# Carrying the count of later neighbours inside the mask chunks of a graph layer

## The chip, the core and the metric

The kernel runs on one core of one Trainium2 chip. Its engines work side by side and wait for one another through semaphores: TensorE (PE, matrix products into the accumulators of PSUM, eight banks), VectorE (DVE), ScalarE (ACT), GpSimd (POOL) and SyncE (SP, which here only issues DMAs). Each engine works through its own instructions in the order in which they were written, and a DMA belongs to the queue of the engine that issues it. The metric is the device time of one execution in microseconds, as the median of the runs.

## The reference

Four graph layers over 4096 nodes with 64 features share one adjacency matrix of 0 and 1 (about one entry in a thousand is 1). Each layer adds to `x` what it computes from `h = max(layernorm(x), 0)`. Layer 0 is an attention with sigmoid scores, masked by the adjacency; layer 2 forms `A h`; layer 3 the mean over the neighbours and a product with a weight matrix. The change concerns layer 1:

```python
support = input @ weight
mask = (adj != 0).astype(support.dtype)
rank = jnp.cumsum(mask, axis=1)
deg = rank[:, -1:]
k = jnp.minimum(deg, 100.0)
pos = rank - (deg - k)
w = mask * jnp.where(pos > 0, 0.5 ** (k - pos), 0.0)
out = w @ support + bias
```

So a neighbour's weight is 0.5 to the power of the number of neighbours that come after it in its row, and nothing if a hundred or more do.

## The kernel before

The adjacency lies transposed in memory, neighbours on the partitions. A block `ib` is 512 of the nodes (8 blocks, `IB`); a chunk `t` is 128 of the possible neighbours (32 chunks, `NT`). In layer 0 POOL's DMAs bring the matrix in as fp8, one tile `masks[ib]` of 128 x 32 x 512 per block, and the later layers use these tiles. Since they hold exact values only for an adjacency of 0 and 1, DVE also checks every chunk in fp32: `check(2)` (L347) issues a load of two chunks (`ckw`, 512 KB) on SP and puts the comparison on DVE; four buffers let the loads run ahead. Should one entry be odd, a general version (`model(True)`) runs afterwards; it doesn't here. A list of checks is worked off in layers 0 to 3 wherever the program calls for one; what is left before the end is done in `done3` (L1545).

*Work in small pieces.* What belongs to the rows of a block (norms, splits, transposes) is written as generators. `push` puts one into a queue with a lag and `step()` (L312) moves each one piece on; the loops of products call `step()` at fixed places. So all engines' instructions have a fixed order, and `manual_schedule` keeps it.

*Layer 1* computes the weights from counts. With h split in two fp16 parts (`s2a`, written by `rows0`), it needs for each chunk and block the number of later neighbours of every entry:

1. `chunks_counted` (L1188) counts, for four blocks at a time (a `quad`), the neighbours in each of the 32 chunks: 128 narrow products into one bank, 32 rows per block. Every eighth chunk it may call a check and calls `step()`. ACT copies the counts into `many` (L1313) and, half by half, into a second tile in which the halves are exchanged (L1317).
2. The loop at L1334 goes through four pairs of blocks, chunks from the last to the first, two chunks a step, so four units (block, chunk) a step and 16 steps a pair. `counted` (L1253) makes for each unit a full product `after` x mask (L1260), 128 times 100 for the entry itself less 128 for every later one in the chunk. Behind the four of them stands a second product for each (L1270), which subtracts the later chunks' counts: its weights are one column of `later` broadcast, 32 rows high, so the four use different rows of the PE array. The units of a step are chosen, with the exchanged tile, so that they do.
3. `weights` (L1277) turns each count into int16, negative ones into 0, on ACT or DVE: the second unit always on DVE, the fourth in every fourth step. Read as bf16 the integer is the power of two that is wanted. The five banks in `COUNTS` take the counts in turn, so a new count waits until the one five units before it has been read.
4. `products` (L1293) multiplies the step before's weights with `s2a` into one of two banks per pair (L1298); after the last chunk ACT evacuates the sum and `rows1` (L1166) goes on with the block's rows.

The loop's line L1343 asks for a check in three of four steps (none in the first four). Layer 2 and 3 are run by `sums` (L1386): 256 products each, a `beat()` (L1360) after every four, with `step()` and, by the pattern `often`, a check. In layer 2 the pattern is two in five; layer 3 begins with one in three and goes over to two in three 24 beats later. `rows2` (L1410) norms the rows for layer 3 and transposes them on PE (L1435), which reads what DVE wrote (L302).

## Time and profile before

| | us |
|---|---|
| median of 3 runs | 595.43 (595.21 to 595.67) |
| span of the profiled execution | 593.2 |
| PE busy in it | 577.5 |
| DVE busy | 477.9 |
| ACT busy | 337.7 |
| layer 1, counting of the chunks | 297.5 to 312.1 |
| layer 1, loop from the first products on | 314.8 to 458.6 |
| layer 2 | 458.6 to 523.8 |
| layer 3 and the end | 523.8 to 593.2 |

Of the profiled execution the span is known: the time from its first to its last instruction; what a run takes besides is the difference to the times of the runs. A row of a group or of the timeline names the engine, the line (L1260), the operation, what it writes and reads (`cnt<-mask,after`), the shapes and how often; then follow its time and, in brackets or behind a bar, the idle time before it with what ended it. PEld is PE's loading of weights, SPq SP's queue. A window's row gives each engine's busy time in it, PEclk the share of the clock that TensorE was granted, and the DMA engines' share. Idle time of an engine costs only where another one waits for it.

### The profile page before, as it was taken

To read this page: it belongs to the slowest core of one execution; us is meant where nothing else is said; L and a number is where in the kernel's file an instruction comes from. 1 tells how busy PE (TensorE), PEld (TensorE's weight loads), DVE (VectorE), ACT (ScalarE), POOL (GpSimd) and SP (SyncE) were. 2 spreads that over 40 slices of the span, in tenths; PEclk is the share of its full clock that TensorE was granted. 3 is DMA by queue.
4 is the path that set the end of the run, shared out by engine and by line. 5 is a ranking of instruction groups with operands and counts; after the bars stand their busy time and mean duration, and the time that the engine had idled before them with its cause. 6 is when DMAs were issued, how large, how long until landed. Compare 5 with 4: busy or idle time off the path is not lost.

```text
span 593.2 us, 9215 instructions
## 1 busy us (share of the span) xinstructions
PE 577.5 (97%) x3138; PEld 238.6 (40%) x3138; DVE 477.9 (81%) x909; ACT 337.7 (57%) x546; POOL 242.7 (41%) x459
## 2 busy tenths in 40 slices
PE   8999999999999999999999999999998999999995
PEld 3663333333333333333243343343443545544553
DVE  5679666899989899999876878879888669987753
ACT  3678666667676776767427677767666014431221
POOL 7625204657767676744434201001010305562352
PEclk9999999999999999999999999999999999999999
DMA  9995932898999899962191545555555486546921
GB/s 148 131 106 45 102 30 18 82 151 136 168 150 166 144 158 153 149 145 88 42 349 38 173 153 189 167 173 177 166 191 181 151 271 200 161 172 210 312 83 42
DMA packets 43016, 87.04 MB, mean 147 GB/s; under 512 B 5136, under 2 KB 22032, under 8 KB 42960
## 3 DMA queue, kind: packets, MB, share of 16 engines
q1 hardware_dynamic: 23808, 68.40, 35.3%
q0 software_dynamic: 18720, 17.57, 31.8%
q8 instruction: 26, 0.43, 0.3%
q10 hardware_dynamic: 432, 0.40, 0.3%
q14 instruction: 30, 0.25, 0.1%
HBM read 135.63 MB, written 1.05 MB: 230 GB/s over the span
## 4 chain that ended last, share of the span: by engine, by line
PE 77%; DVE 10%; POOL 6%; issue 3%; ACT 3%; DMA 1%; DVEq 0%; POOLq 0%; ACTq 0%
PE acc L1370 19%; PE ps L938 12%; PE acc L969 11%; PE acc L1298 10%; PE cnt L1260 9%; DVE att L962 4%; PE cnt L1270 3%; PE idle L1062 3%; PE many L1193 2%; PE pt L236 2%; POOL mask L180 1%; PE pr L1173 1%; POOL rs_a L265 1%; DVE ck L361 1%; PE pn L1447 1%
## 5 line engine op out<-in xcount | busy, mean ns | idle before, releaser
L361 DVE SCALAR_TENSOR_TENSOR ckw<-ckw 128x1024 f32<-128x1024 f32 x98 | 124.5, 1278 | 5.5 <-DMA ckw<-adjt_dram 5.3
L938 PE MATMUL ps<-qt,kt 64*128 64x512 f32 x512 | 123.2, 610 | 2.9 <-DVE att L962 2.5
L969 PE MATMUL acc<-att,fb 128*64 128x512 f32 x512 | 117.8, 599 | 0.6 <-DVE att L962 0.5
L1286 ACT ACTIVATE w<-cnt 128x512 int16<-128x512 f32 x176 | 93.1, 597 | 42.3 <-PE cnt L1270 41.9
L962 DVE TENSOR_TENSOR att<-ps,mask 128x1024 f32<-128x1024 f32 x82 | 98.4, 1217 | 8.4 <-ACT ps L951 8.3
L951 ACT ACTIVATE ps<-ps,att_c,att_a 128x1024 f32<-128x1024 f32 x82 | 93.5, 1177 | 1.5 <-PE ps L938 1.3
L951 ACT ACTIVATE att<-ps,att_c,att_a 128x1024 f32<-128x1024 f32 x46 | 54.6, 1203 | 59.0 <-PE ps L938 58.8
L180 POOL DMA_DIRECT2D mask<-adjt_dram x128 | 70.1, 558 | 19.7 <-DMA mask<-adjt_dram 18.2
L938 PEld LDWEIGHTS ps<-qt,kt 64*128 64x128 f32 x512 | 45.1, 186 | 77.9 <-issue 32.9
L1284 DVE TENSOR_SCALAR w<-cnt 128x512 int16<-128x512 f32 x80 | 53.6, 687 | 23.2 <-PE cnt L1270 21.8
L962 DVE TENSOR_TENSOR att<-att,mask 128x1024 f32<-128x1024 f32 x46 | 56.6, 1246 | 18.1 <-ACT att L951 18.1
L1260 PE MATMUL cnt<-mask,after 128*128 128x512 fp8e4 x256 | 66.3, 379 | 1.9 <-DVE w L1284 1.4
L1298 PE MATMUL acc<-w,s2a 128*128 128x512 bf16 x256 | 66.5, 382 | 0.1
L280 POOL TENSOR_TENSOR xc<-x_sb,st 128x256 f32<-128x256 f32 x24 | 20.0, 832 | 110.1 <-DVE st L277 70.8
L969 PEld LDWEIGHTS acc<-att,fb 128*64 128x64 f32 x512 | 33.5, 136 | 73.0 <-issue 67.5
L1370 PE MATMUL acc<-mask,s2a 128*128 128x512 fp8e4 x256 | 57.8, 379 | 0.0
L1370 PE MATMUL acc<-mask,s2b 128*128 128x512 fp8e4 x256 | 57.7, 379 | 0.0
L265 POOL TENSOR_TENSOR rs_a<-rs_y 128x4 f32<-128x4 f32 x48 | 18.2, 378 | 69.2 <-DVE rs_y L261 66.7
L361 DVE SCALAR_TENSOR_TENSOR ck<-ck 128x512 f32<-128x512 f32 x60 | 43.1, 718 | 0.0
L1260 PEld LDWEIGHTS <-after 128*128 128x128 bf16 x256 | 24.8, 99 | 30.8 <-issue 3.4
L1370 PEld LDWEIGHTS <-s2b 128*128 128x128 f16 x256 | 25.0, 98 | 27.6 <-issue 0.8
L1370 PEld LDWEIGHTS <-s2a 128*128 128x128 f16 x256 | 24.6, 98 | 27.3
(198 smaller groups left out, 606.3 us busy)
## 6 DMA issues: line engine op xcount, KB each, us to landing
ckw<-adjt_dram SPq DMA_DIRECT2D x98, 512.0 KB, 3.5
mask<-adjt_dram POOLq DMA_DIRECT2D x128, 128.0 KB, 9.0
ck<-adjt_dram SPq DMA_DIRECT2D x60, 256.0 KB, 5.9
x_sb<-x_dram SPq DMA_DIRECT2D x4, 256.0 KB, 7.7
out_dram<-y POOLq DMA_DIRECT2D x6, 128.0 KB, 2.2
out_dram<-y ACTq DMA_DIRECT2D x2, 128.0 KB, 2.2
w_sb<-wts_dram SPq DMA_DIRECT2D x2, 80.0 KB, 7.6
vec<-vecs_dram ACTq DMA_DIRECT2D x1, 130.5 KB, 6.3
```

The source lines that it names most:

```text
L180: nc.gpsimd.dma_start(out=masks[ib][:, g * CG : (g + 1) * CG, :], in_=adjt[ib, g])
L265: nc.gpsimd.tensor_tensor(a, y, y, ALU.mult)
L361: nc.vector.scalar_tensor_tensor(at, at, 0.0, at, ALU.not_equal, ALU.not_equal, accum_out=odd[:, k : k + 1])
L938: nc.tensor.matmul(ps[:, c, :], kt[half, g, :], qts[ib][half, :], start=True, stop=True)
L951: nc.scalar.activation(to, ps, AF.Sigmoid, bias=att_c, scale=att_a)
L962: nc.vector.tensor_tensor(att, frm, mask, ALU.mult)
L969: nc.tensor.matmul(acc[c * D : (c + 1) * D, :], lhs[:, t, :], rhs[:, c, :], start=(at == 0), stop=(at == NG - 1), skip_group_check=True,)
L1260: nc.tensor.matmul(cnt, after, masks[ib][:, t, :], start=True, stop=True, skip_group_check=True)
L1284: nc.vector.tensor_scalar(w, cnt, 0.0, None, ALU.max)
L1286: nc.scalar.activation(w, cnt, AF.Relu)
L1298: nc.tensor.matmul(accs[ib], both(s2a, t), w, start=(t == NT - 1), stop=False, skip_group_check=True,)
L1370: nc.tensor.matmul(acc, both(s2, t), masks[ib][:, t, :], start=(t == 0), stop=(t == NT - 1), skip_group_check=True,)
```

## The change

The last two rows of every mask chunk (126 and 127, `LANES`) no longer hold neighbours in layer 1 but two fp8 numbers whose sum is the number of later neighbours, up to 120; `after` has -128 in these rows, so the one product with the mask subtracts them too and the row-tiled product goes. The rows taken out form a 33rd chunk `apart_m` per block (32 chunks x 2 rows, and beneath them the same numbers again), with its own matrix `apart` and its own features `apart_s`. In detail:

- `taken`: for each of the 8 blocks two DMAs on SP copy the two rows (512 bytes x 32 chunks on one partition) to 32 partitions of `apart_m`, at the start of layer 1.
- `numbered`, per quad, replaces the second ACT copies: PE forms the later counts (`beyond` x `many`, and four `pair` products that add the taken rows), DVE makes the two fp8 numbers, and 16 DMAs on SP write them into the mask rows and `apart_m`. Quad 0's runs during the second `chunks_counted`, quad 1's in the loop's first three steps.
- The loop runs over 33 chunks in steps of four units (66 units a pair, so a last step of two); a check comes in every second step from the sixth on, over all pairs. `features_apart` copies two rows of `s2a` by two DMAs when all blocks' features are ready.
- `given_back`: after each pair two DMAs per block restore the mask rows for layers 2 and 3.
- Layer 2's checks go from two in five beats to one in two; the remaining ones before the flag come one a step.
- The constants grow in `count_constants`: small POOL operations, with one more `yield`; `later` goes.

```diff
@@ count_constants
-    nc.vector.tensor_scalar(later[lanes, :], tri[lanes, lanes], -128.0, None, ALU.mult)
+    nc.gpsimd.tensor_scalar(beyond[lanes, lanes], tri[lanes, lanes], 1.0, None, ALU.mult)
...
+            nc.vector.memset(after[:, KEPT:P], 0.0)
...
@@ flagged
+            steps = 7
+            while checks:
+                check(2)
+                steps = max(steps - 1, 3)
+                yield
...
@@ chunks_counted(quad, meanwhile)
                     step()
+                    next(meanwhile, None)
...
+        def lanes_of(ib, n):
+            return masks[ib][KEPT + n : KEPT + n + 1, :, :]
+
+        def taken(ib):
+            for n in range(LANES):
+                nc.sync.dma_start(out=apart_m[n * NT : (n + 1) * NT, ib, :], in_=lanes_of(ib, n))
+
+        def given_back(ib):
+            for n in range(LANES):
+                nc.sync.dma_start(out=lanes_of(ib, n), in_=apart_m[n * NT : (n + 1) * NT, ib, :])
+
+        def numbered(quad):
+            pn = pm.tile([P, IB], F32, tag="pr", name=f"pn_{quad}{sfx}")
+            nc.tensor.matmul(
+                pn, beyond, many[quad], start=True, stop=False, skip_group_check=True
+            )
+            for q in range(QUAD):
+                nc.tensor.matmul(
+                    pn[q * NT : (q + 1) * NT, :], pair, apart_m[:, quad * QUAD + q, :],
+                    start=False, stop=q == QUAD - 1, skip_group_check=True,
+                )
+            yield
+            two = work1.tile([P, LANES, IB], FP8, name=f"two_{quad}{sfx}")
+            nc.vector.tensor_scalar(two[:, 0, :], pn, MOST, None, ALU.min, saturate=False)
+            nc.vector.scalar_tensor_tensor(
+                two[:, 1, :], pn, MOST, two[:, 0, :], ALU.min, ALU.subtract,
+                saturate=False,
+            )
+            yield
+            for q in range(QUAD):
+                ib = quad * QUAD + q
+                rows = slice(q * NT, (q + 1) * NT)
+                for n in range(LANES):
+                    nc.sync.dma_start(out=lanes_of(ib, n), in_=two[rows, n, :])
+                    to = slice((LANES + n) * NT, (LANES + n + 1) * NT)
+                    nc.sync.dma_start(out=apart_m[to, ib, :], in_=two[rows, n, :])
+
+        def features_apart():
+            for n in range(LANES):
+                nc.sync.dma_start(
+                    out=apart_s[n * NT : (n + 1) * NT, :],
+                    in_=s2a[KEPT + n : KEPT + n + 1, :, :, :].rearrange("p t k d -> p t (k d)"),
+                )
@@ counted
+                by, what = (apart, apart_m[:, ib, :]) if t < 0 else (after, masks[ib][:, t, :])
+                nc.tensor.matmul(cnt, by, what, start=True, stop=True, skip_group_check=True)
...
-                nc.tensor.matmul(
-                    cnt, later[lanes, t : t + 1].to_broadcast([NT, P]),
-                    many[ib // QUAD][other][lanes, :],
-                    start=False, stop=True, skip_group_check=True,
-                )
@@ the loop
+            nc.gpsimd.memset(apart_m[LANES * NT : P, :, :].bitcast(I32), 0)
+            nc.gpsimd.memset(apart_s[LANES * NT : P, :], 0.0)
+            for ib in range(NIB):
+                taken(ib)
...
             for blocks in GROUPS:
-                for k in range(NT // PAIR):
-                    t = NT - 1 - k * PAIR
-                    units = [(ib, t - n) for n in range(PAIR) for ib in blocks]
-                    cnts = counted(units)
-                    ws = weights(units, cnts, k)
+                units = [(ib, t) for t in reversed(range(-1, NT)) for ib in blocks]
+                for at in range(0, len(units), CI):
+                    now = units[at : at + CI]
+                    cnts = counted(now)
+                    ws = weights(now, cnts, k)
                     if late is not None:
                         products(*late)
-                    late = units, ws
-                    if k % 4 != 1 and (blocks != GROUPS[0] or k >= 4):
+                    late = now, ws
+                    if k % 2 and k >= 4:
                         check(2)
+                    k += 1
                     step()
+                    next(numbers, None)
+                    if not moved and len(ready.get(1, ())) == NIB:
+                        features_apart()
+                        moved = True
+                if not general:
+                    push(giving(blocks), 2)
...
-        made, beats, often = [0], [0], [True, False, True, False, False]
+        made, beats, often = [0], [0], [True, False]
...
-                    while checks:
-                        check(2)
```

## The prediction, made before the change was run

> **What bounds the kernel now.** I read the page first: TensorE (PE) is busy for nearly the whole span, and the chain that ended last is 77% PE.
>
> ```profile
> span 593.2 us, 9215 instructions
> ...
> PE 577.5 (97%) x3138; PEld 238.6 (40%) x3138; DVE 477.9 (81%) x909; ACT 337.7 (57%) x546; POOL 242.7 (41%) x459
> ...
> PE 77%; DVE 10%; POOL 6%; issue 3%; ACT 3%; DMA 1%; DVEq 0%; POOLq 0%; ACTq 0%
> ```
>
> That share is a mean over stages, so next the stages: layer 1's loop, from its first products to layer 2, and the second half of layer 2.
>
> ```profile
> core 0: us, PE busy (x) PEld busy (x) DVE busy (x) ACT busy (x) POOL busy (x), PEclk, DMA share, GB/s
> 314.80:458.60 143.80, 141.82 (x806) 56.08 (x803) 121.13 (x232) 101.00 (x196) 18.07 (x33) 1.00 0.51 165
> ...
> 488.00:523.80 35.80, 35.80 (x206) 18.83 (x205) 34.22 (x75) 14.71 (x43) 19.84 (x22) 1.00 0.58 180
> ```
>
> PE sets the loop, with VectorE (DVE) at 84% behind it; in layer 2's second half both are full. Then one step of the loop, in order of time:
>
> ```profile
> 343.05 1.04 PE L1298 MATMUL acc<-w,s2a 128*128 128x512 bf16 x4
> ...
> 343.93 1.03 PE L1260 MATMUL cnt<-mask,after 128*128 128x512 fp8e4 x4
> ...
> 344.88 0.10 PEld L1270 LDWEIGHTS <-later 32*128 32x128 bf16 x4 [0.42 <-issue]
> 344.89 0.39 PE L1270 MATMUL cnt<-many,later 32*128 32x512 bf16 x4
> ...
> 345.21 1.04 PE L1298 MATMUL acc<-w,s2a 128*128 128x512 bf16 x4
> ```
>
> A step lasts 345.21 - 343.05 = 2.16 us. A full product takes 0.216 us (in layer 2 twenty in a row took 4.32), so four counts and four products are 1.73 and the row-tiled set is the remaining 0.43: its four run side by side, but their weights load only 0.1 before them and the next weights wait for them.
>
> Then the queue that the change loads, SyncE's (SP): a line's DMA rows, and its first issues of layer 1.
>
> ```profile
> L357 SPq DMA_DIRECT2D ckw<-adjt_dram x98: 327/328/430, 295.4 to 564.0; - x98
> DMA to landing us min/median/max: 3.1/3.5/6.5
> ...
> 295.43 1.75 SPq L357 DMA_DIRECT2D ckw<-adjt_dram  x4
> ```
>
> An issue takes 0.33 us and four come in 1.75: 0.44 each. Last, how closely layer 2's PE follows DVE: the normed rows and the transposes that read them.
>
> ```profile
> 508.37 0.42 DVE L302 SCALAR_TENSOR_TENSOR sup<-xc,rs 128x256 f32<-128x256 f32 x1
> ...
> 514.43 0.42 DVE L302 SCALAR_TENSOR_TENSOR sup<-xc,rs 128x256 f32<-128x256 f32 x1
> ...
> 520.50 0.42 DVE L302 SCALAR_TENSOR_TENSOR sup<-xc,rs 128x256 f32<-128x256 f32 x1
> ```
>
> ```profile
> 509.40 0.38 PE L1435 MATMUL ph<-ident,sup 128*128 128x128 f32 x2
> ...
> 515.16 0.38 PE L1435 MATMUL ph<-ident,sup 128*128 128x128 f32 x2
> ...
> 521.07 0.41 PE L1435 MATMUL ph<-ident,sup 128*128 128x128 f32 x2
> ```
>
> DVE needs 6.06 us a block, PE 5.76, and PE's lead shrinks: from the end of `sup` to the transpose 0.6, 0.3, 0.15 us. There is no slack left for more DVE work.
>
> **The change, part by part.** The sum is made against the profiled span, 593.2; the median of the runs, 595.43, is 2.2 above it, which I take as unchanged.
>
> *Opening of layer 1.* `taken` puts 16 DMAs on SP ahead of the checks' loads: 16 x 0.44 = 7.0 us. Their target lies, by the order of the pools, where layer 0's `kt` was, whose last reader ends at 288.4; SP's last `ck` load goes out at 286.6. So they end at 295.4, just when the first `ckw` load went out before (295.43): nothing, if that reading holds (else the third rival). The memsets on POOL (0.31 for 256 columns, so some 1.2) fall into its idle 296.1 to 303.5. PE then meets `numbered(0)` behind the first four matmuls of the second count: ACT's copy of the counts ended at 305.9, PE is there at 305.4, and five matmuls follow: +1.1, so the counts end at 313.2 instead of 312.1. The two DVE operations stand behind `xc` (L302), which waited for POOL's rsqrt and ended at 309.98; at 0.65 each (the `w` row has 0.687) they end at 311.3. SP issues from 311.4: the first block's second lane is the third DMA (312.2), the second block's the seventh (314.0); landing is taken as 2.2 (the `out_dram` row, the only one from SBUF), so PE may count at 314.4 and 316.2. Four counts, `numbered(1)`'s 0.6, four counts: first products at 318.4 instead of 314.8. **+3.6.** Bounds: +1.7 (only PE's own work) to +5.5 (0.6 an issue, the small L82 loads' row, and 3.1 to land, the `ckw` row's least).
>
> *The loop.* 62 more sets of 0.43 go: **-26.7**; the 33rd chunk adds 8 counts and 8 products of 0.216: **+3.5**.
>
> *SP's queue in the first steps.* `numbered(0)`'s 16 issues last till 318.4. `numbered(1)`'s DVE part runs behind step 1's two `w`, to 320.5; its 16 issues end at 327.6. The load for the check of step 5 is next in that queue: it lands 3.5 later, 331.1. DVE, in order, reaches that check at 326.3 (steps of 1.73) and stands 4.8; behind it is step 6's `w`, ready at 332.8, and its bank is what step 7's third count takes, due at 328.4: **+4.4**. Bounds: 0 (if DVE's slack and shorter issues cover it) and 7.5 (0.6 an issue). `features_apart` does the same again: it waits on SP for the last `s2a` (step 12), two issues, then the load of step 13's check lands 4.4 after `s2a` while DVE is there after 2.0; the bank ring covers 0.4: **+2.0** (0 to 2.5). `given_back` puts four issues (1.8 us) behind each pair of blocks; the loads run four checks, eight steps of 1.73, ahead, which covers it; without that cover DVE waits up to those 1.8 a group.
>
> *DVE and ACT at the faster step.* Thirteen checks at 1.2 leave the loop: DVE has 121 - 16 + 4 = 109 of some 120 us, ACT 101 + 2 (DVE and ACT get four more `w` each for the 33rd chunk, at 0.6 and 0.5; DVE also 1.3 for `numbered(1)`). A step with two `w` and a check is 2 x 0.61 + 1.14 = 2.4 of DVE against 1.73, the next 0.6; five banks let a `w` be 0.8 late. Row work of 2.85 a block lands on top, and at each pair's end two evacuations (1.27 of ACT) meet the next pair's first products, without a row-tiled set between. The loop had 143.8 - 108.9 - 26.7 - 5.8 (row matmuls) = 2.4 of waits; I take 4.5, **+2.1**: nearer the lower end (-2.4) since the slack covers most, the upper being all row work of six blocks uncovered, +15.
>
> *Layers 2 and 3.* They get the 13 checks. Layer 2's 64 beats carry 32 instead of 25; in the stretch from 488 a cycle of five beats gets 2.5 instead of 2, four more in all, at 1.55 each (1.63 and 1.53 beside POOL, 1.22 alone): 6.2 us on a full DVE, less the 0.5 of lead: **+5.7**. Their loads are hidden: the DMA engines are 58% busy there, and a load is issued four checks ahead. Bounds 0 and 7 x 1.55 = 10.9. Layer 3's six lie beside PE, whose transposes there wait for ACT's copies; the last check comes nine beats later, near 574, `flagged` still sums seven steps before its product, and the flag was written at 582: nothing; if DVE lags by more, what passes 582.
>
> *Layer 0.* Thirteen small POOL operations (0.19 as L267) and three memsets (0.1 to 0.23), 3 us, fall into POOL's idle 109.3 to 113.4; DVE loses four of 0.17 in a place (108.6 to 110.2) that the chain passes: **-0.3** (-0.7 to +1). The four ACT copies that go (0.62) were off the path: nothing.
>
> Sum: 3.6 - 26.7 + 3.5 + 4.4 + 2.0 + 2.1 + 5.7 - 0.3 = -5.7: span 587.5, time **589.7**.
>
> *Rule against row.* The Trainium skill, "TensorE: Matmul & The Clock Gate", Part 3, has row-tiled matmuls running side by side, four ending some 4 ns apiece after one. By it a set would cost 0.22, the loop would save 13.6, and the sum would be +7, slower; this trace shows 0.43 a set, which decides. The skill's "SBUF — State Buffer", Door 1, puts partitions 124 to 127 on one of 16 DMA ports, of 435 GB/s together: an estimate of 0.6 us for each 16 KB lane; `taken` would last 9.6 instead of 7.0 us and the sum would be -3; no row here shows a transfer from one partition.
>
> **The rivals.**
> - *The queue waits are hidden and layer 2 keeps up* (loads early enough, DVE's extra checks in its idle time of early layer 2): the 4.4, 2.0 and most of the 5.7 go: 578 to 585. For it: DVE idles 10 us from 458 to 488. Against it: order in a queue is fixed, and the stretch from 488 is full.
> - *DVE and ACT become the loop's bound*: a step of 1.85 instead of 1.73 over 66 steps, +8 on the sum: 594 to 600. For it: DVE at 91% with lumps of 2.4; against: 13 checks fewer.
> - *Slower: SP's queue at the opening.* If `apart_m` is free only when the last gather ends (295.4), the 7.0 us of `taken` stand before the first `ckw`: the checks on DVE, `xc` behind them, both numbers and their DMAs come 6.6 later, so 589.7 + 6.6 = 596.3, and with issues of 0.6 instead of 0.44 (2.6 more on `taken`, 3 on step 5) 602. It decides from a delay of 7 us. For it: the first `ckw` load itself waited for that gather. Against: its pool lies further up, over `att`.
>
> **How the numbers follow.** Forecast 0.45 (585 to 594), hidden 0.17, DVE and ACT 0.15, SP's queue 0.23. A measurement tells 0.2%, 1.2 us, from no change: faster is below 594.2, the first two, 0.62; same is where the last two begin, 0.08; slower the rest, 0.30. Leaving out a tenth at each end gives 580 to 602. Low are the hidden case's middle, high the slower rival's end.
>
> **What would show it.** A step of 1.73 us without L1270; PE idle some 3 us before the first counts, released by a DMA; DVE waiting for `ckw` loads near steps 5 and 13; transposes L1435 that wait for `sup` in layer 2, and a longer layer 2. I'm wrong if the 16 `taken` issues begin after 295, if DVE doesn't wait for `ckw` in the loop, if the step stays near 2 us, or if PE's idle time lowers the granted clock: it stayed 1.00 over 1.7 us of idle at 295.4.

## The result and the profile after

The changed kernel is slower: 620.43 us median of 4 runs (618.69 to 623.11) against 595.55, a ratio of 1.0417, 95% interval 1.0391 to 1.0444. The forecast was 589.7, with 602 as its upper end. The profiled execution has a span of 617.0 us (before 593.2). From the same marks in both traces, with the forecast's own terms beside them:

| stretch | before | after | difference | forecast |
|---|---|---|---|---|
| up to the first counting product | 297.5 | 298.1 | +0.6 | -0.3 |
| opening: counting to the loop's first products | 17.3 | 38.2 | **+20.9** | +3.6 |
| loop of layer 1 | 143.8 | 133.4 | -10.5 | -14.7 |
| layer 2 | 65.2 | 69.5 | +4.3 | +5.7 |
| layer 3 and the end | 69.4 | 77.8 | **+8.4** | 0 |
| span | 593.2 | 617.0 | +23.8 | -5.7 |

The page of the changed kernel: PE was busy for 97% before, now for 91%, and the chain that ended last, 77% PE before, is 47% PE; the rest is other engines, DMAs and queues.

```profile
span 617.0 us, 8858 instructions
...
PE 562.3 (91%) x2916; PEld 240.1 (39%) x2916; DVE 482.4 (78%) x914; ACT 337.4 (55%) x546; POOL 257.3 (42%) x477
...
PE 47%; DVE 21%; POOL 10%; issue 7%; DMA 7%; ACT 4%; SPq 3%; DVEq 0%; POOLq 0%; ACTq 0%
```

The stretches by windows (busy time of each engine, PE's granted clock, DMA share): the opening's late part, the loop, the second half of layer 2, layer 3 up to the flag, and the end.

```profile
core 0: us, PE busy (x) PEld busy (x) DVE busy (x) ACT busy (x) POOL busy (x), PEclk, DMA share, GB/s
314.80:336.30 21.50, 4.62 (x13) 1.24 (x14) 10.01 (x21) 3.32 (x7) 11.01 (x29) 0.60 0.20 68
336.30:469.70 133.40, 121.37 (x578) 56.80 (x577) 106.22 (x208) 100.75 (x197) 14.14 (x27) 0.99 0.38 131
503.50:539.20 35.70, 31.95 (x182) 16.32 (x180) 34.15 (x77) 13.71 (x41) 24.63 (x22) 1.00 0.68 232
539.20:602.00 62.80, 57.93 (x300) 28.62 (x298) 48.67 (x92) 15.45 (x40) 26.47 (x25) 1.00 0.67 228
602.00:617.00 15.00, 7.48 (x30) 3.44 (x30) 4.33 (x14) 0.47 (x1) 2.02 (x3) 0.75 0.10 33
```

In 314.8 to 336.3, where the kernel before had PE busy throughout, PE worked for 4.6 of 21.5 us, at 0.60 of its clock. In the loop it was idle for 12 of 133 us. The opening in order of time, first SP's queue:

```profile
297.13 10.88 SPq L1288 DMA_DIRECT2D apart_m<-mask  x16
308.12 6.36 SPq L362 DMA_DIRECT2D ckw<-adjt_dram  x6
326.24 0.55 SPq L1318 DMA_DIRECT2D mask<-two  x1
```

then DVE's first check before the change and its work after it, and PE's wait behind both:

```profile
298.85 1.23 DVE L361 SCALAR_TENSOR_TENSOR ckw<-ckw 128x1024 f32<-128x1024 f32 x1 [0.20 <-DMA ckw<-adjt_dram]
```

```profile
311.50 1.22 DVE L366 SCALAR_TENSOR_TENSOR ckw<-ckw 128x1024 f32<-128x1024 f32 x1 [12.22 <-DMA ckw<-adjt_dram]
...
323.28 0.92 DVE L307 SCALAR_TENSOR_TENSOR xc<-xc,rs_y 128x256 f32<-128x256 f32 x1 [2.59 <-POOL rs_y L273]
...
325.53 0.68 DVE L1308 TENSOR_SCALAR two<-pn 128x512 fp8e4<-128x512 f32 x1
```

```profile
329.74 0.61 PE L1338 MATMUL cnt<-mask,after 128*128 128x512 fp8e4 x1 [15.65 <-DMA mask<-two]
332.28 1.46 PE L1338 MATMUL cnt<-mask,after 128*128 128x512 fp8e4 x3 [1.93 <-DMA mask<-two]
```

The lanes (`taken`) begin at 297.13 and hold SP until 308.0, so the first check load goes out at 308.12 instead of 295.43. DVE's first check of layer 1 starts at 311.50 (before: 298.85), the other five and the row work follow in the order written, and the numbers, whose inputs PE had ready at 307.4, are made at 325.5. A step of the loop is what the forecast said, 1.73 us (424.08 - 422.36 = 1.72 for a count set to the next):

```profile
422.36 1.03 PE L1338 MATMUL cnt<-mask,after 128*128 128x512 fp8e4 x4
423.22 1.03 PE L1363 MATMUL acc<-w,s2a 128*128 128x512 bf16 x4
424.08 0.59 PE L1338 MATMUL cnt<-mask,after 128*128 128x512 fp8e4 x2
```

Layer 2's normed rows, which came every 6.06 us before, now come every 6.06 and 6.85 us in turn (516.18 to 523.03 is a long one):

```profile
516.18 0.43 DVE L307 SCALAR_TENSOR_TENSOR sup<-xc,rs 128x256 f32<-128x256 f32 x1
...
523.03 0.43 DVE L307 SCALAR_TENSOR_TENSOR sup<-xc,rs 128x256 f32<-128x256 f32 x1
...
529.09 0.43 DVE L307 SCALAR_TENSOR_TENSOR sup<-xc,rs 128x256 f32<-128x256 f32 x1
```

In layer 3, DVE in order of time: every block's cycle of 5.2 us holds two checks and a wait for POOL. Before the change the cycle was the same, and the last check began at 573.16:

```profile
562.73 1.22 DVE L361 SCALAR_TENSOR_TENSOR ckw<-ckw 128x1024 f32<-128x1024 f32 x1
...
567.95 1.22 DVE L361 SCALAR_TENSOR_TENSOR ckw<-ckw 128x1024 f32<-128x1024 f32 x1
...
573.16 1.22 DVE L361 SCALAR_TENSOR_TENSOR ckw<-ckw 128x1024 f32<-128x1024 f32 x1
...
581.40 4.49 PE L1370 MATMUL acc<-mask,s2a 128*128 128x512 fp8e4 x20
```

After it:

```profile
578.68 0.43 DVE L1551 TENSOR_TENSOR y<-y,rdegs 128x256 f32<-128x256 f32 x1 [1.71 <-POOL y L249]
579.03 1.22 DVE L366 SCALAR_TENSOR_TENSOR ckw<-ckw 128x1024 f32<-128x1024 f32 x1
580.17 1.75 DVE L366 SCALAR_TENSOR_TENSOR ckw<-ckw 128x1024 f32<-128x1024 f32 x1
581.85 0.41 DVE L1558 SCALAR_TENSOR_TENSOR y<-y,x_sb 128x256 f32<-128x256 f32 x1
583.91 0.43 DVE L1551 TENSOR_TENSOR y<-y,rdegs 128x256 f32<-128x256 f32 x1 [1.65 <-POOL y L249]
```

The end, in order of time: DVE's last check, the sum over the checks, PE's product for the flag, which waits 4.57 us, and the twenty last products, 6.18 us instead of the 4.49 above.

```profile
600.64 1.21 DVE L366 SCALAR_TENSOR_TENSOR ckw<-ckw 128x1024 f32<-128x1024 f32 x1
601.89 0.42 DVE L1185 TENSOR_REDUCE bad<-odd 128x1 f32<-128x256 f32 x1
...
602.37 0.19 PE L1189 MATMUL pf<-one,bad 128*1 128x1 f32 x2 [4.57 <-DVE bad L1185]
602.49 6.18 PE L1445 MATMUL acc<-mask,s2a 128*128 128x512 fp8e4 x20
```

### The profile page after: what moved, and what is told of

Its sections match the earlier page's. It is cut to its first block, busy times and chain, and to the rows that moved or that the text cites. A ratio compares the mean times of both kernels' runs of the same rounds, so it can differ in the third digit from the quotient of the medians.

```text
span 617.0 us, 8858 instructions
## 1 busy us (share of the span) xinstructions
PE 562.3 (91%) x2916; PEld 240.1 (39%) x2916; DVE 482.4 (78%) x914; ACT 337.4 (55%) x546; POOL 257.3 (42%) x477
## 4 chain that ended last, share of the span: by engine, by line
PE 47%; DVE 21%; POOL 10%; issue 7%; DMA 7%; ACT 4%; SPq 3%; DVEq 0%; POOLq 0%; ACTq 0%
PE acc L989 12%; PE ps L958 11%; PE cnt L1338 7%; PE acc L1363 7%; DVE ckw L366 7%; PE acc L1445 4%; DMA ckw<-adjt_dram 4%; DVE att L982 3%; DVE w L1349 2%; POOL mask L185 2%; SPq L1288 2%; DMA w_sb<-wts_dram 1%; POOL rs_a L270 1%; POOL y L1555 1%; ACT ps L971 1%
## 5 line engine op out<-in xcount | busy, mean ns | idle before, releaser
L1338 PE MATMUL cnt<-mask,after 128*128 128x512 fp8e4 x256 | 69.8, 389 | 27.2 <-DMA mask<-two 17.6
L285 POOL TENSOR_TENSOR xc<-x_sb,st 128x256 f32<-128x256 f32 x24 | 22.0, 915 | 111.0 <-DVE st L282 71.5
L1445 PE MATMUL acc<-mask,s2a 128*128 128x512 fp8e4 x256 | 59.4, 387 | 0.0
L1363 PEld LDWEIGHTS <-s2a 128*128 128x128 f16 x256 | 25.3, 99 | 32.5 <-issue 3.4
L1445 PEld LDWEIGHTS <-s2a 128*128 128x128 f16 x256 | 25.1, 99 | 28.6 <-issue 2.3
```

What stands on the lines that cost most here:

```text
L1338: nc.tensor.matmul(cnt, by, what, start=True, stop=True, skip_group_check=True)
L1363: nc.tensor.matmul(accs[ib], apart_s if t < 0 else both(s2a, t), w, start=(t == NT - 1), stop=False, skip_group_check=True,)
L1445: nc.tensor.matmul(acc, both(s2, t), masks[ib][:, t, :], start=(t == 0), stop=(t == NT - 1), skip_group_check=True,)
```

## The experiments

My theory after this reading: the removal of the row-tiled products works as forecast, and three things take more than it gives: the opening (check loads behind the lanes in SP's queue, and the numbers behind the checks on DVE), SP's queue in the loop's first twenty steps, and the 13 checks that went to layers 2 and 3. Every run below is an edit of the changed kernel; the diffs of the last three are shown against the run before them. The table has the marks of each profile (us) and the times against the kernel before.

| run | first products | layer 2 | layer 3 | span | median | ratio (95%) |
|---|---|---|---|---|---|---|
| before | 314.8 | 458.6 | 523.8 | 593.2 | 595.55 | 1 |
| changed | 336.3 | 469.7 | 539.2 | 617.0 | 620.43 | 1.0417 (1.0391 to 1.0444) |
| lanes behind the loads | 325.7 | 459.4 | 529.2 | 607.2 | 610.23 | 1.0256 (1.0236 to 1.0277) |
| no checks in the opening | 317.9 | 451.6 | 522.3 | 601.6 | 603.83 | 1.0145 (1.0108 to 1.0182) |
| numbers first | 331.6 | 464.9 | 535.0 | 612.6 | 614.99 | 1.0332 (1.0313 to 1.0350) |
| lanes early | 337.5 | 474.1 | 543.3 | 619.9 | 621.60 | 1.0444 (1.0401 to 1.0488) |
| own pool | 336.8 | 470.4 | 542.5 | 619.9 | 619.58 | 1.0390 (1.0352 to 1.0429) |
| filler | 335.9 | 472.4 | 540.9 | 617.6 | 619.32 | 1.0398 (1.0378 to 1.0419) |
| queue in the loop | 336.0 | 461.1 | 533.9 | 611.5 | 610.26 | 1.0242 (1.0223 to 1.0260) |
| even steps | 335.3 | 470.0 | 541.0 | 618.4 | 624.48 | 1.0495 (1.0451 to 1.0539) |
| 13 checks fewer | 336.0 | 469.4 | 534.6 | 605.1 | 607.22 | 1.0215 (1.0185 to 1.0245) |
| flag late | 336.1 | 469.3 | 541.2 | 617.6 | 619.91 | 1.0423 (1.0394 to 1.0452) |
| all together | 323.6 | 454.2 | 519.8 | 596.4 | 598.54 | 1.0042 (1.0027 to 1.0057) |
| all, mended | 321.6 | 451.1 | 517.0 | 590.6 | 590.50 | 0.9902 (0.9884 to 0.9921) |
| all, mended twice | 316.7 | 449.5 | 515.4 | 588.3 | 589.71 | 0.9898 (0.9869 to 0.9928) |
| that, own pool | 322.6 | 451.3 | 517.2 | 591.0 | 594.30 | 0.9986 (0.9965 to 1.0007) |

**The opening: who holds the numbers?** The 16 lane transfers behind the check loads:

```diff
-            for ib in range(NIB):
-                taken(ib)
...
+            def first_taken():
+                yield
+                yield
+                yield
+                for ib in range(QUAD):
+                    taken(ib)
...
-            laid(0, chunks_counted(0, iter(())))
-            numbers = numbered(0)
+            laid(0, chunks_counted(0, first_taken()))
+            numbers = second_taken(numbered(0))
```

> The changed kernel with one thing moved: the 16 DMAs of taken stand behind the check loads in SP's queue (eight behind the first four loads, eight behind the sixth) instead of ahead of them all. Theory (SP's order at the opening: the loads come late, DVE waits for them, and the two operations that make the numbers stand behind that wait): first check near 300.5 instead of 311.5, the numbers near 313 instead of 325.5, first products of the loop near 322 instead of 336.3, time 605 to 609. Rival (the number DMAs themselves and their landing set the opening, whatever stands ahead): first products stay after 333, time over 617.

The first products came at 325.7, 10.6 us earlier, and the time was 610.23: the order of SP's queue is half of the opening's loss. The theory had 322 and at most 609: the first check came as expected (300.2), but the fifth stood 2.4 us for its load, which was behind eight lanes, and the numbers were made at 314.9. Then the six checks of the opening left out, the lanes where the change has them:

```diff
-                        check(2)
+                        checks.popleft()
+                        checks.popleft()
```

> The changed kernel without the six checks of the opening (they are left out, so 12 of the 256 chunks aren't checked); the 16 DMAs of taken stay where they are. Theory (DVE's wait for the late loads holds the numbers): SP is free at 308, the numbers come behind xc near 311, first products near 321, time 603 to 608. Rival (SP's own 10.9 us of issues or the number DMAs set the opening, with or without checks): first products after 330, time over 615.

Here the lanes hold SP from 297.5 to 308.6, no less than in the changed kernel, and still the numbers are made at 308.4 and the first products stand at 317.9:

```profile
308.35 0.68 DVE L1309 TENSOR_SCALAR two<-pn 128x512 fp8e4<-128x512 f32 x1
```

```profile
315.77 0.82 PE L1339 MATMUL cnt<-mask,after 128*128 128x512 fp8e4 x3 [1.01 <-DMA mask<-two]
...
317.94 1.03 PE L1364 MATMUL acc<-w,s2a 128*128 128x512 bf16 x4
```

So the 11.1 us of issues do not hurt by themselves: DVE does, which works in the order written and stands at checks whose loads are late. That 317.9 is so near the forecast's 318.4 is partly luck: the six checks' own 7.3 us of DVE left with their waits, the numbers ended 1.5 us earlier than in the forecast (309.8, not 311.3), and the way from there to the products took 1.1 longer. The third way round, one line moved, so that the numbers stand ahead of the beat's check and row step on DVE:

```diff
+                    next(meanwhile, None)
                     if quad == 0 or t < NT // 2:
                         check(2)
                     step()
-                    next(meanwhile, None)
```

> Edit: one line of the changed kernel moved: in the beats of the counting the numbers' step is emitted ahead of the check and the row step of the same beat; nothing else, so SP's queue is as it was. Theory A (the numbers are late because VectorE takes its work in the order written, and late check loads stand ahead of them): they now stand behind five checks instead of six and the row step, are made at about 321 instead of 327, the first products of the loop stand 5 to 7 us earlier (329.5 to 331.5) and the time is 613 to 616. Rival B (the row chain of the last block, now behind the numbers, holds the loop instead): 618 or more.

The numbers were made at 320.4, the first products came at 331.6, and the time was 614.99: a line's place was worth 5 us.

How much was the storage, which the forecast had wrong? Two runs. The first gave the lanes storage of their own and issued them at the end of layer 0:

```diff
-        apart_m = parts_b.tile([P, NIB, IB], FP8, name="apart_m" + sfx)
+        apart_m = main.tile([P, NIB, IB], FP8, name="apart_m" + sfx)
...
-        ATTS = 2 if general else 6
+        ATTS = 2 if general else 5
```

> Edit: the tile of lanes lies in storage of its own from the start, and the 16 lane transfers are issued at the end of layer 0's queue, as the prediction had assumed; to make room, layer 0 has five instead of six buffers for masked attention tiles. Theory A (the storage was the first cause of the late opening: SP's transfers could not begin before 297.1; VectorE's wait for check loads behind them was what it cost): the lane transfers are issued between 288.6 and 299, the opening's check loads follow by 299 instead of 308, the numbers are made near 314.5 instead of 326, the loop's first products stand 10 to 13 us earlier (323 to 326) and the time is 607 to 611. Theory B (the storage was all that the prediction had wrong in the opening): first products at 318 to 320, time 602 to 604. Rival C (the storage did not matter; the 16 issues block the check loads wherever they stand): 616 or more.

621.60: by the time alone rival C. But the buffer taken from layer 0 lengthened that: counting began at 306.73 instead of 298.09. Against that start, 8.6 later, the transfers (298.02 to 309.33) began at 289.4, near the forecast's 288.4; the numbers (327.06) came 7.1 and the first products (337.53) 7.4 us earlier than in the changed kernel, less than theory A's 10 to 13 and far from theory B. The subtraction assumes that the longer layer 0 changed nothing else. The second run was meant to show it without that side effect, with a pool of its own for the lanes:

```diff
-        apart_m = parts_b.tile([P, NIB, IB], FP8, name="apart_m" + sfx)
+        apart_p = pool("apart", 1)
+        apart_m = apart_p.tile([P, NIB, IB], FP8, name="apart_m" + sfx)
```

> Edit: the tile of lanes gets a pool of its own, opened between those of layer 1's features and of the check loads; nothing else moves, layer 0 included, and the 16 lane transfers stay where they are in SP's queue. Its storage is then that of layer 0's kt, as the prediction had assumed for the changed kernel. Theory A (the transfers were late through their storage, but their 16 issues of 0.6 to 0.7 us take the check loads' place in any case): the issues begin near 288.6 instead of 297.1 and end by 300, the check loads follow 8 us earlier than in the changed kernel but 5 later than in the kernel before, the first products of the loop stand 7 to 9 us earlier, at 327 to 329.5, and the time is 611 to 614. Theory B (the storage was all that went wrong in the opening): first products at 318 to 321, time 602 to 606. Rival C (the storage did not matter): 618 or more.

It told nothing of that kind: 619.58, and SP's queue stood as before, because the first lane waited for layer 0's last product (`acc`, the gather of the forecast) all the same:

```profile
SPq L1290 <- PE acc L989: 8.2, 1, 8.2
```

(Who waits, what for, us in all, times, longest.) So what was taken to be `kt`'s storage is not free there either, and how the compiler laid these pools was not found out. What stands is the first run, with its side effect taken off by subtraction: by it some 7.4 of the 21 us were the storage, and the rest was there with it free.

Last, PE's clock. PE idled for 15.7 us; the granted clock fell to 0.5 and stayed there until 336.3, 6.6 us after the work began:

```profile
314.10:318.00 3.90, 0.00 (x0) 1.00 0.97 371
318.00:322.00 4.00, 0.00 (x0) 0.66 0.05 22
322.00:329.70 7.70, 0.00 (x0) 0.50 0.04 9
329.70:334.00 4.30, 2.32 (x5) 0.50 0.12 29
334.00:338.00 4.00, 3.38 (x13) 0.71 0.09 21
```

(Windows of PE in the changed kernel: busy time, clock, DMA share, GB/s.) Filler products kept it busy:

```diff
+                for _ in range(64):
+                    nc.tensor.matmul(
+                        idle, after, masks[2 * QUAD - 1][:, 0, :], start=True, stop=True,
+                        skip_group_check=True,
+                    )
```

> Edit: 64 products of mask chunks by the triangle into a spare bank, read by nobody, stand on TensorE behind the second quad's counting, where TensorE was idle for 15.7 us; at full clock they take 64 x 0.216 = 13.8 us; nothing waits for them but TensorE's own next work. Theory A (the idle time lowers the granted clock to 0.5, and the loop's first counts and products run at half speed between 329.7 and 336.3): the granted clock stays near 1.0, some 17 matmuls gain about 0.2 us each, the first products of the loop stand 2 to 3.5 us earlier and the time is 617 to 618.5. Rival B (the landings of the numbers and VectorE set that stretch, and the half clock is hidden behind them): less than 0.7 us, 619.7 or more.

The clock stayed at 1.00 up to 329.5, the first products came at 335.9, 0.4 earlier, and the time, 619.32, can't be told from the changed kernel's. That is near rival B's less than 0.7, but it doesn't settle the price of the half clock, since the edit did not keep the clock up where it mattered. PE stood again for 1.3 and 2.1 us at the landings, and from 332 to 334 the granted clock was 0.50: the three counts behind the second landing took the same 1.46 us as in the changed kernel.

```profile
332.08 1.46 PE L1338 MATMUL cnt<-mask,after 128*128 128x512 fp8e4 x3 [2.14 <-DMA mask<-two]
```

Only the last four counts were faster (1.38 us instead of 1.86). An estimate from the changed kernel's rows: PE worked without a wait from 332.28 to 336.33 at a clock of 0.50, and half of these 4.05 us, 2.0, is what the full clock would save. No run shows it. In the loop's waits the clock fell as well (0.94 in 345 to 375, 0.85 with the fillers).

**The loop: SP's queue.** The second quad's transfers spread, the features' on POOL's queue:

```diff
             for q in range(QUAD):
+                if q:
+                    yield
+                    yield
...
-                nc.sync.dma_start(
+                nc.gpsimd.dma_start(
```

> Edit: the second quad's 16 number transfers leave SP one block (four of them) every second step of the loop instead of all 16 behind one another, and the two transfers of the features go out on POOL's queue instead of SP's; the rest as in the changed kernel. Theory A (what holds PE between 336 and 375 is check loads that stand in SP's queue behind the number transfers, 338.4 to 348.8, and behind the features' transfers, where SP waits 14.6 us for DVE's s2a): VectorE's waits for check data there (8.9 us in two) go, PE's idle time between 336 and 375 falls from 9.8 us to 3 to 5, and the time falls by 4 to 7 us, to 613 to 616. Rival B (the row chain of the last block and the waits between DVE and POOL hold the loop's first twenty steps anyway): less than 1.5 us, 619 or more.

The loop fell from 133.4 to 125.1 us, and the median by 10, more than expected. DVE's waits for check data in the loop, in the changed kernel and in this run:

```profile
DVE ckw L366 <- DMA ckw<-adjt_dram: 8.2, 2, 5.5
```

```profile
DVE ckw L366 <- DMA ckw<-adjt_dram: 2.1, 2, 1.4
```

Theory A: the wait of 5.5 us behind the numbers' transfers fell to 1.4, and the one of 2.8 behind the features' is gone. Layer 2 was 3 us longer in this profile, which is the longest of the five runs, so the profile's gain is 5.5 where the medians differ by 10. The other edit in the loop moved the checks to the even steps, away from those with two weight tiles on DVE:

```diff
-                    if k % 2 and k >= 4:
+                    if k % 2 == 0 and k >= 4:
```

> Edit: in the loop of layer 1 the checks stand in the even steps, in which VectorE makes one of the four weight tiles, instead of the odd ones, every second of which has two; the same number of checks but one more. Theory A (the loop's late part is bound by the row sets' removal alone, PE busy 92.4 of 94.7 us, and VectorE's lumps of 2.7 us in one step cost at most the 2.3 us that are idle): 0 to 2 us less, 618.5 to 620.5. Rival B (VectorE, 87% busy there, holds the loop in lumps all along, early part included): 4 us less or more, 616 or less.

It was slower, 624.48, which neither theory had: the first check is now step 4's, its load still stands behind the second quad's transfers, and DVE waits longer for it, with PE behind (8.4 us in one wait, 5.5 in the changed kernel):

```profile
350.93 1.22 DVE L366 SCALAR_TENSOR_TENSOR ckw<-ckw 128x1024 f32<-128x1024 f32 x1 [7.88 <-DMA ckw<-adjt_dram]
```

It speaks for the queue again. What DVE's lumps cost is not shown by it; from 375 on PE was idle for 2.8 us, before the edit for 2.3. In this profile the loop is only 1.3 us longer than in the changed kernel's, so where the median's other 3 us went stays open.

**The late checks.** The 13 checks left out (26 of 256 chunks unchecked), layer 2's pattern as before:

```diff
-        made, beats, often = [0], [0], [True, False]
+        made, beats, often = [0], [0], [True, False, True, False, False]
+        for _ in range(0 if general else 26):
+            checks.popleft()
```

> The changed kernel with the 13 checks that it moved to layers 2 and 3 left out (26 of 256 chunks aren't checked) and layer 2's old pattern of two in five beats. Theory (the moved checks make DVE too slow for PE's transposes in layer 2, and the flag's product at the end waits for them): layer 2 goes back from 69.5 to 65.2 us and the part after it from 77.8 to 69.4, time 606 to 609. Rival (layers 2 and 3 are longer from something else, the given-back rows or the clock): no more than 4 us less, time over 616.

Layer 2 took 65.2 us, exactly as before the change, layer 3 and the end 70.5 instead of 77.8, and the time was 607.22. The checks are 11.6 of the 12.7 us that these two stretches had lost. The flag's product put behind the last product, so that PE no longer waits for it:

```diff
-            for _ in range(steps):
+            while made[0] < 2 * NIB * NT:
                 yield
```

> The changed kernel with the flag's product behind the last product of layer 3 instead of twenty products ahead of it. Theory (PE stands 4.6 us there for DVE's sum over the checks, and then runs at half the clock for some nine products, 1.9 us): time 613 to 615, PE without a wait in the last 30 us. Rival (the end is set by DVE's checks and the output rows anyway): time 619 or more.

A miss: 619.91. PE's wait was nearly gone (0.27 us) and its last product of the layer ended 6.5 us earlier, counted from layer 3's start, but layer 3 and the end took 76.4 us instead of 77.8, hardly less than the 76.6 to 78.0 of other runs with the same layer 3. ACT's last evacuation stands right behind ACT's output of the block before (608.90 to 609.26), whose row DVE finished at 608.87, and DVE came to that row only behind its last checks and their sum:

```profile
603.86 0.42 DVE L1185 TENSOR_REDUCE bad<-odd 128x1 f32<-128x256 f32 x1
...
608.79 0.14 DVE L1190 TENSOR_SCALAR flag<-pf 1x1 int32<-1x1 f32 x1
609.36 0.48 ACT L1572 ACTIVATE asb<-acc,level 128x256 f32<-128x256 f32 x1 [9.79 <-DVE flag L1190]
```

The profile puts ACT's wait down to the flag, which DVE wrote at the same moment. So most of the 4.57 us on PE had no price of its own: DVE's backlog sets the end on the other path too.

**Put together.** The opening's, the loop's and the layers' remedies in one kernel:

```diff
+                    by = nc.scalar if at % 2 and not (quad or h) else nc.sync
+                    by.dma_start(out=lanes_of(quad * QUAD + q, n).bitcast(F32), in_=two[rows, n, :].bitcast(F32))
...
-                    if k % 2 and k >= 4:
+                    if k >= 4 and (k % 2 == 0 or (k % 8 == 7 and k > 8)):
...
-        made, beats, often = [0], [0], [True, False]
+        made, beats, often = [0], [0], [True, False, True, False, False]
```

> Edit: all that the runs so far point to, together. The first quad's eight lane transfers go half on SP, half on ACT ahead of everything else; the numbers are emitted ahead of the check and the row step of their beat; of the first quad's numbers only the four lane transfers that the loop's first steps read go out before the loop, half on SP, half on ACT; all other transfers of numbers and the second quad's eight lane transfers follow in the loop, two in a step; the features' transfers go out on POOL's queue; the loop's checks stand in even steps, and one more in every eighth step; layer 2 has its old rate of checks again, 2 in 5 beats. Theory A (the losses are the order of transfers and of VectorE's work in the opening, SP's queue in the loop, and the 13 checks that went to layers 2 and 3, where VectorE is the bound): first products of the loop 316 to 319, loop 122 to 128 us, layer 2 65 to 66.5, layer 3 and the end 69 to 71, time 577 to 586, faster than before. Rival B (the shorter step itself makes VectorE and ACT the bound of the loop, so that the checks can't be put back): loop 130 us or more and the time 588 to 597.

598.54: 22 us won, level with the kernel before but for 0.4%. Of theory A's marks only layer 2 came (65.6). The first products were late (323.6), since the first check still stood at 305.0, behind four lanes in SP's queue. The loop took 130.6 us, which is rival B's 130 or more: from 350 to 358 DVE waited three times for late check loads, with PE behind it (0.7, 1.1 and 3.1 us) and then at a clock of 0.61 (358 to 366). Layer 3 and the end took 76.6, with the last check 61.6 us after layer 3's start. That was mended (check loads ahead of the lanes, the numbers out before the lanes go back, the checks spread more evenly):

```diff
+            def first_sent():
+                yield
+                yield
+                yield
+                for ib in range(QUAD):
+                    lane_sent(ib, 0, nc.sync)
...
+            laid(0, chunks_counted(0, first_sent()))
...
-            often[:] = [True, False, False]
+            often[:] = [True, False, True, False, True, False, False]
```

> Edit: as the run with everything together, with four things mended. In SP's queue four check loads of the opening stand ahead of the first quad's lane transfers again (half of these on ACT), where the kernel before had them; the second quad's lane transfers follow in the opening, so that all its numbers are out by the loop's 17th step, ahead of the transfers that give the lanes back after the first group; the loop's additional checks begin at step 23 instead of 15; layers 2 and 3 have 3 checks in 7 beats instead of 2 in 5 and 1 in 3. Theory A (what was left of the loss is the opening's late check loads, first products at 323.6 instead of 314.8; the stall and half clock of 351 to 364, where SP waited for its own earlier transfers; and the check backlog at the end, flag at 583.4): first products 316 to 319, loop 121 to 126 us, layer 3 and the end 68 to 72, time 578 to 587, faster than before. Rival B (DMA bandwidth and VectorE hold checks and weights in any order): 592 or more.

590.50, 1% below the kernel before, but neither theory's time, and three marks of theory A were missed: first products at 321.6, loop 129.5, layer 3 and the end 73.6. In the opening DVE stood 4.56 us at the fifth check, with the numbers behind. So the fifth and sixth went to the loop:

```diff
-                    if quad == 0 or t < NT // 2:
+                    if quad == 0:
                         check(2)
```

> Edit: as the mended run with everything together, but the opening's fifth and sixth check are taken out of VectorE's queue ahead of the numbers (they follow in the loop, whose checks begin at step 2), and four of the second quad's lane transfers move behind the first numbers. Theory A (what is left of the opening's loss is the fifth check, whose load was late: VectorE waited 4.6 us for it with the numbers behind): the numbers are made by 309 instead of 314.4, the loop's first products stand at 316 to 318 instead of 321.6 and the time is 584 to 588. Rival B (the lost checks come back as waits in the loop or at the end): 589 to 592.

The numbers were made at 308.1, the first products stood at 316.7, as theory A had it, and the time, 589.71, hardly moved, as rival B had it. That it equals the forecast's 589.7 is chance: the loop is 3.7 us longer than forecast, layer 3 and the end 3.5, layer 2 5.0 shorter. A window of this run's loop:

```profile
375.00:450.00 75.00, 72.24 (x341) 34.37 (x346) 71.18 (x140) 61.16 (x122) 9.02 (x11) 1.00 0.47 158
```

PE is busy for 72.2 and DVE for 71.2 of these 75 us; which of the two would bound the loop, no run shows. The loop takes 132.8 us instead of the 125.1 of the run with seven checks fewer, and of the 11.3 us in which PE stood in it 8.5 lie ahead of 375, where DVE waited 6.5 us at two check loads and PE 1.9 us for the features. The last run sent the first eight lanes ahead of the check loads, all on SP, into the pool of their own:

```diff
             for ib in range(QUAD):
-                lane_sent(ib, 1, nc.scalar)
+                for n in range(LANES):
+                    lane_sent(ib, n, nc.sync)
```

> Edit: as the mended run without the fifth and sixth check of the opening, with the pool of the run beside it: the first quad's eight lane transfers go out on SP ahead of the check loads, and none on ACT. Theory A (with the storage free the eight transfers lie in layer 0's last microseconds and cost nothing, and the check loads come as in the kernel before): first check at 299 to 300.5, first products of the loop at 315.5 to 317, time 586 to 589. Rival B (the eight issues still delay the first check by 3 us or more, and the numbers with it): first products at 318 or later, 590 or more.

594.30, rival B: the lanes went out from 296.5 to 301.5, the first check stood at 305.2, the first products at 322.6.

## Why the prediction was wrong

*The opening, +3.6 forecast, +20.9 measured: the step that failed.* Two statements in it. First the storage: "their target lies, by the order of the pools, where layer 0's `kt` was". SP waited from 288.6 to 297.1, and a lane took 0.68 us with its gap instead of 0.44: the lanes ended at 308.0, not 295.4 (8.7 from the start, 3.9 from the pitch). Second, what stands behind them: the forecast had DVE's numbers wait only for the row work, although the same six checks stand ahead of them; their loads had moved by 12.7 us and everything on DVE with them. From the first check to the end of the numbers DVE took 15.4 us where 12.5 were reckoned. Of these 3.0 us 0.5 is a misreading (the row of `xc` before ends at 309.56 + 0.92 = 310.5, not at 309.98), 1.4 the row work that stands between `xc` and the numbers, and the rest came with the late loads. From there to the first products it took 9.4 instead of 7.1: 0.4 up to PE's second landing (issues of 0.63 instead of 0.44), 1.9 from there, where PE ran at a clock of 0.50. 12.65 + 3.0 + 2.3 = 17.9, which is 336.3 less the forecast's 318.4. The run without these checks shows which of the two carries the loss: with the same late lanes the opening took 19.5 us, near the 20.9 forecast.

The third rival had this mechanism, with a chance of 0.23 and a time of 596 to 602. It was sized by a shift of 6.6 us, 9.2 at its upper end with issues of 0.6; measured were 12.7, since layer 0's last product ended at 297.0 and not at 295.4, and a lane took 0.68. The place was right and the size too small, and it had nothing for layer 3.

*The loop, -14.7 forecast, -10.5 measured.* Right in kind: the step is 1.73 us, so 0.43 a set, and DVE did stand at two late check loads (5.5 and 2.8 us). The two queue terms, 4.4 + 2.0, were worth 8.3 us in the profile of the run that took them out. With them out the loop stood at -18.7, where the forecast without them has -21.1.

*Layer 2, +5.7 forecast, +4.3 measured.* Right in kind, a little large: every second cycle was longer by 0.8 us, and without the 13 checks the layer is as before. Profiles of kernels with the same layer 2 lie between 68.5 and 72.8 us, so the 1.4 between the two is no finding.

*Layer 3, nothing forecast, +8.4 measured: the second failed step.* It said that the last check comes nine beats later, near 574, and that only what passes 582 costs. But 574 is where the kernel before already had its last check (573.16 + 1.22 = 574.4). Counted from layer 3's start it ended after 50.6 us before the change (574.4 - 523.8) and after 62.6 with it (601.9 - 539.2): nine beats of four products are 7.8 us, and 12 were measured. The program's place of a check was taken for its time. The program asks for two checks in three beats, 2.6 us; DVE does two in a cycle of 5.2, since its row work waits 1.65 us for POOL each time, and POOL's next piece stands behind an output transfer that waits for DVE's row work behind the two checks. The profile before shows the same cycle (562.73, 567.95, 573.16). The text named the condition ("if DVE lags by more") and gave it no price.

*The clock.* That PE's idle time lowers it was named as a way to be wrong; it happened, and by the estimate above it cost some 2.0 us in the opening. The run with fillers could neither confirm nor exclude that, as its clock had fallen again, and no run kept the clock up at the end, where twenty products took 6.18 us instead of 4.49. The rows above show 0.66 in the second four microseconds of idleness, then 0.50. The Trainium skill, "TensorE: Matmul & The Clock Gate", Part 1 (the two states), has the half clock after at least one idle window of some 3.4 us, which agrees.

*The port.* The forecast gave, beside its sum, 9.6 us for the lanes, an estimate from the Trainium skill, "SBUF — State Buffer", Door 1; measured were 10.9. That is nearer than the 7.0 that was used, but the numbers' transfers between 32 partitions had issues just as long (0.52 to 0.59 us), and so had a check load right behind a copy (0.52 to 0.58), so a port as the cause is not shown.

## What to carry to other kernels

An instruction that is hidden today is hidden by its place in a queue: before a transfer is put ahead of others, ask which engine stands at the later ones, and what is written behind it on that engine. Work moved to a later stage must be placed by the time the engine reaches it there, not by its place in the program. And a rival that is right in kind should be priced to its end: here it was seen that the loads would be late, and their delay was put at half of the 12.7 us.

## What was not expected of the hardware

- A 16 KB copy between partitions took SP longer to issue than a 512 KB load: 0.52 to 0.60 us (one of 1.37) against 0.33, or 0.38 to 0.48 behind another load, and 16 in a row took 10.9 us. The copy's shape is not all of it, since a check load right behind a copy took 0.52 to 0.58 us too, here between two pairs of copies in the loop of the changed kernel:

```profile
437.28 0.53 SPq L362 DMA_DIRECT2D ckw<-adjt_dram  x1
```

- With check loads under way eight such copies took 8.0 us, in the mended run:

```profile
300.09 8.02 SPq L1392 DMA_DIRECT2D apart_m<-mask  x8
```

- From issue to landing the median was 2.3 us from one partition to 32 (the lanes), 2.2 from 32 to one and 1.8 from 32 to 32, less than the 4.3 of a check load in the same run (3.5 before the change).
- The granted clock was 0.50 up to 336.3, 6.6 us after the first work, and 1.00 from there (336.3 to 345.3); PE had been busy for 4.6 of these 6.6 us.
